# One visit per tile: all of layer 0's other matmuls in a single break of the weighing

## The chip, the cores and the metric

The kernel runs on one core of a Trainium2 chip. Times are device microseconds (us) of one execution. The engines are PE (TensorE; PEld is its weight load), DVE (VectorE), ACT (ScalarE), POOL (GpSimd) and SP (SyncE, which issues most DMAs). Each engine works through its own list of instructions in order and waits on semaphores for the others.

## The reference, cut to what matters

Four graph layers, each followed by a residual sum and a layer norm, on x of 8 batches x 2048 nodes x 64 channels with one 2048 x 2048 adjacency A (a 0/1 mask, each row divided by its sum). The change touches layer 0 and the first steps of layer 1:

```python
# layer 0: Chebyshev terms T0 = I, T1 = A, T2 = 2 A A - I
w = jnp.einsum('nd,dkio->nkio', embedding, weight)   # each node's own weights, D = 16, K = 3
b = jnp.einsum('nd,do->no', embedding, bias)
x_g = jnp.einsum('knm,bmc->bnkc', A_stack, x)
out = jnp.einsum('bnki,nkio->bno', x_g, w) + b
x = layernorm(x + out)
# layer 1, its start
h = x @ W
s = leaky_relu(h @ a_node, 0.2)                      # a score per node and batch
alpha = softmax(where(H.T > 0, s, NEG))              # over the nodes of each of 64 hyperedges
agg = einsum('ben,bnf->bef', alpha, h)
beta = sigmoid((h @ a_gn)[..] + (agg @ a_ge)[..])
industry = (adj / deg) @ (x @ W_ind)
```

## The kernel before, in words

Nodes are taken in 16 tiles of 128 (NT = 16). A first stage (`first_product`, matmul at L492) forms y1 = A x for all tiles, as a mask product in which every fp32 operand is split in a high and a low part (`y_hi`, `y_lo`). Layer 0's loop (`layer0`) then runs over the tiles j = 0 to 16 (the last turn only finishes tile 15).

The bulk of a tile is the *weighing* (`weigh`, matmuls L1109, evacuation L1120): per tile 8 groups g0 to g7; a group multiplies x, y1 and y2 of two batch pairs with the weights of four of the 16 embedding dimensions, on half of the array's rows at a time (64 x 128 weights), into one of two PSUM buffers (`pp`); DVE then adds the four results, each scaled by the node's embedding, to the running sum `r` in four scalar_tensor_tensor instructions. All else is put between the groups by hand, in a fixed list (`program_order` chains every engine's instructions in the order in which they are written):

- after g0, g1, g2: the three steps of the layer norm of tile j - 1 (`normed`, L1128 to L1156); after g1 the first half of POOL's mask scaling of tile j + 1 (`scaled`, L1011 to L1022); after g2 `first_terms` of tile j + 1: y1 transposed (4 matmuls L167), the bias term bp (L1053) from a small load `et`, its copy, and r = x + bias on POOL (L1058).
- after g3: `project` of tile j - 2 (8 matmuls L1197: h and the industry features at once; copies L1216, low part L1217; POOL weights h by the exponential of its score, L1224), the product y2 = A y1 of tile j + 1 (32 matmuls L1072, copy L1078), `to_features` of tile j - 1 (4 transposes, copy L1171), the comparison of the scaled mask with A (`compare`, L1027, DVE), the second half of `scaled` on POOL, and the masks of tile j + 2 (`mask`, L1003, DVE, two of 128 x 1024).
- after g5: the second `compare`, and the low part of the weighted h (`low_part`, L1238, POOL).
- after g6: `second_term` of tile j + 1 (4 transposes of y2, L1088), `scores` of tile j - 1 (8 matmuls L1176 with `wa`, then L1181 to L1188 with the exponential), `gather` of tile j - 2 (2 matmuls L1245).
- after g7: `degrees` of tile j + 1 (1 matmul L1094).

PSUM holds one accumulator for the product, one for the gather, two small buffers (tag `tr`) for transposes and the like, and two `pp` buffers of two banks, which weighing and projection take in turn. In `first_product` seven accumulators (`acc`) are passed around, four for each quarter of the nodes. SP issues the loads (adjacency tile, row scales, x transposed, x) and stores of a tile in the written order too.

The lines of the changed functions and of their callers:

Of the kernel before, what the change touches and what calls it, by code (L numbers as in the profile page):

```python
# [62 lines left out]
def kernel(  # L63
# [168 lines left out]
    def load_w0(pool):  # L232
        w_sb = pool.tile([P, K, D * C], F32, tag="w", name="w0_sb")
        for h in range(2):
            nc.sync.dma_start(w_sb[h * 64:(h + 1) * 64], w0)
        emb_sb = pool.tile([P, NT, D], F32, tag="emb", name="emb_sb")
        nc.sync.dma_start(emb_sb, emb.rearrange("(t p) d -> p t d", p=P))
        bias_sb = pool.tile([D, C], F32, tag="bias", name="bias0_sb")
        nc.sync.dma_start(bias_sb, bias0)
        return w_sb, emb_sb, bias_sb  # L240
# [183 lines left out]
    def first_product(own, pre, rawp, mskp, y_hi, y_lo, prepare):  # L424

        x_hi, x_lo = buffer(own, 0, "x_hi"), buffer(own, 1, "x_lo")
        with tc.tile_pool(name="acc0", bufs=7, space=PSUM) as ps_acc, tc.tile_pool(
# [14 lines left out]

            steps = prepare(ps_s)
# [33 lines left out]
            with program_order():  # L477
                begin(0)
                begin(1)
                for n, (q, i, kk, h) in enumerate(pieces):  # L480
                    begin(n + 2)
                    if i + h == 0:
# [3 lines left out]
                        ]  # L486
                    m = m_of.pop(n)
# [468 lines left out]
    def layer0(  # L956
        own, l0s, rawp, mskp, ps_acc, ps_tr, ps_p, w_sb, emb_sb, bias_sb, bad, deg, y_hi, y_lo,
# [5 lines left out]
        h_sb, wb, wa, vecs, av_sb, pm, es, hgr, aggp, rden, early = layer1s  # L963
        raws, msk, terms, resid, norm, srow = {}, {}, {}, {}, {}, {}
        x1s, xTs, hps, hss, mds = {}, {}, {}, {}, {}

        homes = {"xT": (0, 1, 2), "xs": (3, 4), "hs": (5,), "hsf": (15,), "y1T": (6, 7), "r": (8, 9),
# [23 lines left out]
        def load_x(j):  # L991
            ncols = slice(j * P, (j + 1) * P)
            xT = tile("xT", f"xT_{j}", (P, NP, P))
            nc.sync.dma_start(xT, xt[:, :, ncols])
            et = tile("et", f"et_{j}", (D, P))
            nc.sync.dma_start(et, embt[:, ncols])
            xs = tile("xs", f"xs_{j}")
            nc.sync.dma_start(xs, xn[ncols, :])
            terms[j] = {"x": xT, "et": et, "xs": xs}
# [31 lines left out]

        def first_terms(j):

            tr = ps_tr.tile([P, NP, P], F32, tag="tr", name=f"try1_{j}")
            if j > 1:
                y1 = tile("y1", f"y1_{j}", bufs=1)
                nc.gpsimd.tensor_tensor(y1, y_hi[:, j, :], y_lo[:, j, :], ALU.add)
            for pr in range(NP):
                pc = slice(pr * P, (pr + 1) * P)
                if j > 1:  # L1040
                    transpose(tr[:, pr, :], y1[:, pc])
# [10 lines left out]
            bp = ps_tr.tile([P, QW], F32, tag="tr", name=f"bp_{j}")  # L1052
            nc.tensor.matmul(bp[:, 0:C], terms[j]["et"], bias_sb, start=True, stop=True)  # L1053
            bn = tile("bn", f"bn_{j}", (P, C))
            nc.scalar.copy(bn, bp[:, 0:C])
            r = tile("r", f"r0_{j}")
            for bq in range(2):
                nc.gpsimd.tensor_tensor(  # L1058
                    r[:, 4 * bq * C:4 * (bq + 1) * C]
                    .rearrange("p (h l c) -> p h l c", h=2, l=2),  # L1060
                    swapped(terms[j]["xs"], bq),
                    bn.rearrange("p (h l c) -> p h l c", h=1, l=1).to_broadcast([P, 2, 2, C]),
                    ALU.add,
                )
            resid[j] = r
# [58 lines left out]
        def normed(j, step):  # L1124
            r = resid[j]
            if step == 0:
                s = tile("s", f"s_l0_{j}", (P, B))
# [7 lines left out]
            elif step == 1:  # L1135
                var = tile("var", f"var_l0_{j}", (P, B))
# [8 lines left out]
                std = tile("std", f"std_l0_{j}", (P, B))  # L1145
# [27 lines left out]
        def scores(j):  # L1173
            sp = ps_tr.tile([P, NP, 2, 2], F32, tag="tr", name=f"sgp_{j}")
            for pr in range(NP):
                nc.tensor.matmul(  # L1176
                    sp[:, pr].rearrange("p i h -> p (i h)"), xTs[j][:, pr, :],
                    wa.rearrange("p i h -> p (i h)"), start=True, stop=True,
                )
            sg = tile("sg", f"sg_{j}", (P, NP, 2))  # L1180
            nc.scalar.copy(sg, sp[:, :, 0, :])  # L1181
            nc.scalar.copy(hgr[:, j, 0, :].rearrange("p (r h) -> p r h", h=2), sp[:, :, 1, :])
            ej = es[:, j, :]
            nc.vector.scalar_tensor_tensor(
                ej.rearrange("p (r h) -> p r h", h=2), sg, 0.2, sg, op0=ALU.mult, op1=ALU.max
            )
            nc.vector.tensor_scalar(ej, ej, TOP, None, op0=ALU.min)
            nc.scalar.activation(ej, ej, AF.Exp)  # L1188

        def project(j, h_first=False):  # L1190

            mm = ps_p.tile([P, 2, 2, 4 * C], F32, tag="pp", name=f"hp_{j}")
            mm = mm.rearrange("p h l (m x) -> p h (l m) x", m=2)
            for pr in range(NP):
                for h in range(2):
                    rs = slice(h * 64, (h + 1) * 64)
                    nc.tensor.matmul(  # L1197
                        mm[:, h, pr, :], xTs[j][rs, pr, :], wb[rs], start=True, stop=True
                    )
            if j not in mds:  # L1200
                md = tile("md", f"md_{j}", (P, 2, E))
                nc.gpsimd.tensor_copy(r_(md), pm[:, j, :].unsqueeze(1).to_broadcast([P, 2, E]))
                mds[j] = md.rearrange("p h e -> p (h e)")

            def by_half(t):
                return t.rearrange("p (r h c) -> p h r c", h=2, c=C)


            stay = j >= len(kept_i)
            if stay:  # L1210
# [963 lines left out]
```

## Time and profile before

| what | us |
|---|---|
| median of 3 runs | 1312.41 (1310.28 to 1313.22) |
| span of the profiled execution | 1314.5 |
| first product and preparation | 0 to about 154 |
| layer 0's loop, steady tiles: start of product to start of the next | 33.48 (most), 34.44 (one) |
| product starts of the first tiles | 156.23, 179.43, 210.22, 243.13, 276.63 |
| product start of tile 15 / last matmul of the gather | 645.98 / 714.19 |

The profile comes from one execution, whose own time has no row among the three runs; its span of 1314.5 is 2.1 us above their median. A row of the timeline gives start, length, engine, line, operation, output <- inputs, shape and count of merged instructions; in brackets stands how long the engine was idle before and what ended that. "issue" means that it waited for nothing that the profile shows. A row of the windows gives, for a stretch, the busy time of PE, PEld, DVE, ACT and POOL with instruction counts, then the granted PE clock, the DMA engines' share and GB/s. For an in-order engine the start of one instruction to the start of the next is what a chain is made of; lengths overlap a little.

### The profile page before, as it was taken

To read this page: it belongs to the slowest core of one execution; us is meant where nothing else is said; L and a number is where in the kernel's file an instruction comes from. 1 tells how busy PE (TensorE), PEld (TensorE's weight loads), DVE (VectorE), ACT (ScalarE), POOL (GpSimd) and SP (SyncE) were. 2 spreads that over 40 slices of the span, in tenths; PEclk is the share of its full clock that TensorE was granted. 3 is DMA by queue.
4 is the path that set the end of the run, shared out by engine and by line. 5 is a ranking of instruction groups with operands and counts; after the bars stand their busy time and mean duration, and the time that the engine had idled before them with its cause. 6 is when DMAs were issued, how large, how long until landed. Compare 5 with 4: busy or idle time off the path is not lost. (4 is left out here: it accounts for less than half of the span.)

```text
span 1314.5 us, 19978 instructions
## 1 busy us (share of the span) xinstructions
PE 1253.7 (95%) x7692; PEld 1002.0 (76%) x7692; DVE 886.6 (67%) x1596; ACT 377.9 (29%) x852; POOL 514.4 (39%) x418
## 2 busy tenths in 40 slices
PE   7999799999999999999998599999998899999996
PEld 6777578888888888888886367777766788888885
DVE  5455268888887777887673568877774666665544
ACT  3000001222222222222222356666664521111111
POOL 1000274555554555555411468888872600000000
PEclk9999799999999999999997689999998999999998
DMA  8877833323333333332352212223220133334541
GB/s 293 240 210 149 217 94 105 105 102 102 106 107 107 108 107 107 107 106 82 112 187 75 101 65 97 96 96 97 81 96 1 70 124 128 104 122 152 187 173 67
DMA packets 100792, 157.22 MB, mean 120 GB/s; under 512 B 12881, under 2 KB 64465, under 8 KB 94673
## 3 DMA queue, kind: packets, MB, share of 16 engines
q1 hardware_dynamic: 98208, 151.65, 35.8%
q10 hardware_dynamic: 2304, 4.20, 0.8%
q8 instruction: 63, 1.03, 0.3%
q0 software_dynamic: 176, 0.02, 0.1%
q14 instruction: 41, 0.33, 0.1%
HBM read 118.08 MB, written 37.76 MB: 119 GB/s over the span
## 5 line engine op out<-in xcount | busy, mean ns | idle before, releaser
L1120 DVE SCALAR_TENSOR_TENSOR r<-pp,emb_sb,r 128x256 f32<-128x256 f32 x512 | 247.2, 483 | 105.3 <-PE pp L1109 90.4
L1109 PE MATMUL pp<-w_sb,xT 64*128 64x256 f32 x1024 | 160.6, 390 | 1.8 <-DVE r L1120 1.8
L1109 PE MATMUL pp<-w_sb,y1T 64*128 64x256 f32 x1024 | 153.6, 376 | 0.0
L1109 PE MATMUL pp<-w_sb,y2T 64*128 64x256 f32 x1024 | 153.6, 376 | 0.0
L1058 POOL TENSOR_TENSOR r<-xs,bn 128x256 f32<-128x256 f32 x32 | 22.8, 732 | 245.5 <-issue 213.2
L492 PE MATMUL y1p<-x_hi,m 128*128 128x512 f32 x256 | 107.4, 420 | 7.1 <-ACT x_hi L438 7.1
L1109 PEld LDWEIGHTS pp<-w_sb,xT 64*128 64x128 f32 x1024 | 94.5, 186 | 19.7 <-issue 9.6
L1109 PEld LDWEIGHTS pp<-w_sb,y2T 64*128 64x128 f32 x1024 | 99.8, 187 | 10.8
L1109 PEld LDWEIGHTS pp<-w_sb,y1T 64*128 64x128 f32 x1024 | 99.8, 187 | 10.8
L492 PE MATMUL y1p<-x_lo,m 128*128 128x512 f32 x256 | 104.1, 407 | 0.0
L1072 PE MATMUL y2p<-y_hi,msk 128*128 128x512 f32 x256 | 103.0, 402 | 0.0
L1442 PE MATMUL ind<-y_hi,mj_l 128*128 128x512 f32 x240 | 101.7, 424 | 0.0
L1072 PE MATMUL y2p<-y_lo,msk 128*128 128x512 f32 x256 | 101.3, 396 | 0.0
L1442 PE MATMUL a<-v_hi,mj_l 128*128 128x512 f32 x256 | 100.1, 392 | 0.0
L1442 PE MATMUL a<-v_lo,mj_l 128*128 128x512 f32 x256 | 100.0, 391 | 0.0
L1442 PE MATMUL a<-y_lo,mj_l 128*128 128x512 f32 x240 | 95.1, 396 | 0.0
L1442 PE MATMUL a<-y_hi,mj_l 128*128 128x512 f32 x240 | 94.9, 395 | 0.0
L1442 PE MATMUL ind<-y_lo,mj_l 128*128 128x512 f32 x240 | 94.6, 394 | 0.0
L739 POOL TENSOR_TENSOR ez<-ez,coef 128x1024 f32<-128x1024 f32 x32 | 69.9, 2183 | 56.3 <-DVE ez L737 54.9
L1011 POOL TENSOR_TENSOR ms<-msk,srow 128x1024 f32<-128x1024 f32 x32 | 89.8, 2806 | 4.7 <-DVE ms L1027 4.7
L1003 DVE TENSOR_SCALAR msk<-adj 128x1024 fp32r<-128x1024 f32 x32 | 63.6, 2021 | 9.1 <-DMA adj<-in_at 9.0
L492 PEld LDWEIGHTS y1p<-x_hi,m 128*128 128x128 f32 x256 | 50.2, 196 | 19.6 <-ACT x_hi L438 7.1
(286 smaller groups left out, 2430.3 us busy)
## 6 DMA issues: line engine op xcount, KB each, us to landing
mj_l<-mask SPq DMA_DIRECT2D x46, 1024.0 KB, 4.9
raw<-in_at SPq DMA_DIRECT2D x32, 512.0 KB, 5.0
adj<-in_at SPq DMA_DIRECT2D x64, 256.0 KB, 3.9
mask<-msk SPq DMA_DIRECT2D x32, 512.0 KB, 4.6
xraw<-in_xn SPq DMA_DIRECT2D x8, 512.0 KB, 4.6
oh<-oh SPq DMA_DIRECT2D x32, 128.0 KB, 2.8
xT<-in_xt SPq DMA_DIRECT2D x16, 256.0 KB, 3.2
xs<-in_xn SPq DMA_DIRECT2D x16, 256.0 KB, 2.9
```

The costliest lines, as they stand in the source:

```text
L492: nc.tensor.matmul(accs[q][jj], r_(m[:, t, jj * P:(jj + 1) * P]), r_(part[:, mt, :]), start=i + h + t == 0 and part is x_hi, stop=i == 3 a ...
L739: nc.gpsimd.tensor_tensor(by_b(ez), by_b(ez), per_b(coef, 2 * i, 2), ALU.mult)
L1003: nc.vector.tensor_scalar(r_(m), raws[j][h], 0.0, None, op0=ALU.is_gt)
L1011: nc.gpsimd.tensor_tensor(ms, m, srow[j].unsqueeze(1).to_broadcast([P, 8, P]), ALU.mult)
L1058: nc.gpsimd.tensor_tensor(r[:, 4 * bq * C:4 * (bq + 1) * C] .rearrange("p (h l c) -> p h l c", h=2, l=2), swapped(terms[j]["xs"], bq), bn. ...
L1072: nc.tensor.matmul(acc, r_(msk[j, mt // 8][:, mt % 8, :]), r_(part[:, mt, :]), start=mt == 0 and part is y_hi, stop=mt == NT - 1 and part ...
L1109: nc.tensor.matmul(pp[:, h, pl, :], terms[j][name][rs, 2 * bq + pl], w_sb[rs, k, dq * 4 * C:(dq + 1) * 4 * C], start=k == 0, stop=k == K - 1,)
L1120: nc.vector.scalar_tensor_tensor(rb, ppv[:, :, dd, :], emb_sb[:, j, d:d + 1], rb, op0=ALU.mult, op1=ALU.add)
L1442: nc.tensor.matmul(acc, r_(a[:, mt, :]), r_(part[:, mt, :]), start=mt == 0 and part is hi, stop=mt == NT - 1 and part is lo,)
```

## The change

Layer 0's loop now leaves the weighing once per tile, after g3 (`visit`). In that break stand, in this order: the second half of the projection of tile j - 2 and its score weights, the y1 transposes of tile j + 1, the weighting of tile j - 2, the product of tile j + 1, the transposes of x1 of tile j - 1, the gather of tile j - 2, the y2 transposes of tile j + 1, the degrees of tile j, the first half of the projection of tile j - 1, and at the end the masks of tile j + 2.

- `project` is cut in two halves of two batch pairs each, each with its own `pp` buffer; `wb` has two more columns (W a_node and W a_gn), so that the scores come out of the projection and the matmuls of `scores` and `wa` are gone. The exponential (`weights_of`) and the weighting (`weighted`) follow the projection; the low part is formed at once, in the buffer of y1.
- The bias term of all tiles is formed in 16 matmuls ahead of the first product (`node_bias`), from an embedding loaded whole on ACT's DMA queue into buffers that y_lo takes later; its result takes two of the seven `acc` buffers for a while, and is copied by ACT (`keep_bias`). The per-tile loads of `et`, bp and its copy are gone.
- `first_terms` is cut: `begin_terms` (POOL: y1 = high + low, r = x + bias) after g2, the transposes in the visit. `xs` (x of a tile) has one buffer instead of two and is loaded after `begin_terms`; `ihi` takes the freed one.
- At the end of the loop (j = 16) the second half of tile 15's projection, its weights and the last denominators stand after each other; the buffer of the denominators comes from `tr`.

```diff
+            def node_bias():
+                et, bn_all, rest = bias_in
+                b0 = bn_all[0:D, NT - 1, :]
+                for half in range(2):
+                    bp = ps_acc.tile([P, NT // 2, C], F32, tag="acc", name=f"bp_{half}")
+                    for t in range(NT // 2):
+                        j = half * (NT // 2) + t
+                        nc.tensor.matmul(
+                            bp[:, t, :], et[j // 4][0:D, (j % 4) * P:(j % 4 + 1) * P], b0,
+                            start=True, stop=True,
+                        )
+                    bps.append(bp)
+                rest()
...
+                    if n == 0:
+                        node_bias()
+                    elif n == 1:
+                        keep_bias()
...
-        def scores(j):
-            sp = ps_tr.tile([P, NP, 2, 2], F32, tag="tr", name=f"sgp_{j}")
-            for pr in range(NP):
-                nc.tensor.matmul(
-                    sp[:, pr].rearrange("p i h -> p (i h)"), xTs[j][:, pr, :],
-                    wa.rearrange("p i h -> p (i h)"), start=True, stop=True,
-                )
...
+        def project(j, n, h_first=False):
+            mm = ps_p.tile([P, 2, 2, 4 * C], F32, tag="pp", name=f"hp_{j}_{n}")
+            mm = mm.rearrange("p h l x -> p h (l x)")[:, :, 0:2 * (2 * C + 2)]
+            mm = mm.rearrange("p h (r x) -> p h r x", r=2)
+            for r in range(2):
                 for h in range(2):
                     rs = slice(h * 64, (h + 1) * 64)
                     nc.tensor.matmul(
+                        mm[:, h, r, :], xTs[j][rs, 2 * n + r, :], wb[rs], start=True, stop=True
                     )
...
+            nc.scalar.copy(by_batch(sgs[j]), mm[:, :, :, 2 * C])
+            nc.scalar.copy(by_batch(hgr[:, j, 0, :]), mm[:, :, :, 2 * C + 1])
...
+        def weights_of(j):
+            ej, sg = es[:, j, :], sgs[j]
+            nc.vector.scalar_tensor_tensor(ej, sg, 0.2, sg, op0=ALU.mult, op1=ALU.max)
+            nc.vector.tensor_scalar(ej, ej, TOP, None, op0=ALU.min)
+            nc.scalar.activation(ej, ej, AF.Exp)
...
-            hss[j] = tile("hs", f"hs_hi_{j}"), hs
-            nc.scalar.copy(r_(hss[j][0]), hs)
...
+            hi, lo = tile("hs", f"hs_hi_{j}"), tile("y1", f"hs_lo_{j}", bufs=1)
+            nc.scalar.copy(r_(hi), hs)
+            nc.gpsimd.tensor_tensor(r_(lo), hs, hi, ALU.subtract)
+            hss[j] = hi, lo
...
+        def visit(j):
+            when(j - 2, project, 1)
+            when(j - 2, weights_of)
+            when(j + 1, first_terms)
+            when(j - 2, weighted)
+            if j + 1 < NT:
+                for _ in product(j + 1):
+                    pass
+            when(j - 1, to_features)
+            when(j + 1, compare, 0)
+            when(j + 1, scaled, 1)
...
+            when(j - 2, gather)
+            when(j + 1, second_term)
+            when(j, degrees)
+            when(j - 1, project, 0, j == NT)
+            when(j + 2, mask, 0)
+            when(j + 2, mask, 1)
...
                     elif g == 3:
-                        when(j - 2, project)
-                        if j + 1 < NT:
-                            for _ in product(j + 1):
-                                pass
-                        when(j - 1, to_features)
-                        when(j + 1, compare, 0)
-                        when(j + 1, scaled, 1)
...
-                        when(j + 2, mask, 0)
-                        when(j + 2, mask, 1)
+                        visit(j)
                     elif g == 5:
                         when(j + 1, compare, 1)
-                        when(j - 2, low_part)
...
-                    elif g == 6:
-                        when(j + 1, second_term)
-                        when(j - 1, scores)
-                        if j < NT:
-                            when(j - 2, gather)
-                        else:
-                            project(NT - 1, h_first=True)
-                            denominators(NT - 1, NT)
-                            gather(NT - 2)
...
+                    elif g == 6 and j == NT:
+                        project(NT - 1, 1, h_first=True)
+                        weights_of(NT - 1)
+                        weighted(NT - 1)
+                        denominators(NT - 2, NT)
...
-                    elif g == 7:
-                        when(j + 1, degrees)
```

## The prediction

> **What bounds it now.** I read the page's busy shares first, then the span by slices, then busy time by windows.
>
> ```profile
> span 1314.5 us, 19978 instructions
> ...
> PE 1253.7 (95%) x7692; PEld 1002.0 (76%) x7692; DVE 886.6 (67%) x1596; ACT 377.9 (29%) x852; POOL 514.4 (39%) x418
> ...
> PE   7999799999999999999998599999998899999996
> ```
>
> ```profile
> 410.61:444.09 33.48, 33.48 (x267) 28.25 (x265) 26.82 (x50) 7.56 (x15) 17.86 (x15) 1.00 0.32 105
> ```
>
> The window is one tile of layer 0's loop: 33.48 us, all PE, at full clock; DVE has work for 26.82, POOL for 17.86. So an interruption of PE costs its length, and DVE has 6.7 us to spare, but only if it can use them. The timeline of the same tile shows one interruption:
>
> ```profile
> 427.02 0.60 PE L1109 MATMUL pp<-w_sb,y2T 64*128 64x256 f32 x4
> ...
> 427.55 0.42 PEld L167 LDWEIGHTS try<-ident,y 128*128 128x128 f32 x4 [0.33 <-issue]
> 427.55 0.65 PE L167 MATMUL try<-ident,y 128*128 128x128 f32 x4
> ...
> 428.04 0.95 PE L1176 MATMUL sgp<-wa,xT 128*128 128x4 f32 x8
> ...
> 429.49 0.30 PEld L1109 LDWEIGHTS pp<-w_sb,xT 64*128 64x128 f32 x4 [0.36 <-issue]
> 429.49 0.70 PE L1109 MATMUL pp<-w_sb,xT 64*128 64x256 f32 x4
> ```
>
> The reader is to see the engine change from weighing (64 rows) to transposes, scores and gather (128 rows) and back, with "issue" gaps at both ends: nobody is waited for, the change itself takes that time. Weighing matmuls start in pairs, 0.216 us apart (the starts of the rows: 427.02 to 427.24). On leaving, the next start comes after 0.31 (427.24 to 427.55); on return the first pair takes 0.32 (429.49 to 429.81). This interruption thus costs 429.49 - 427.45 (where the next pair would have started) + 0.10 = 2.14. By the same reckoning the four of a tile cost 1.15 (after group g2), 9.07 (after g3), 2.14 (after g6) and 0.40 (after g7), 12.77 in all; eight groups of 12 pairs x 0.2157 = 2.59 us are 20.7. The sum, 33.47, is the tile.
>
> **PE after the change.** T = 0 is the first projection matmul of the only visit. From the rows' starts: half a projection, 4 pairs by 0.11 and 0.21 to the next kind, 0.54; y1 transposes to 1.1; product 7.22 from first to last start, so 8.3; transposes of x1 to 8.9; the gather's two at 9.0 and 9.3. Here sits the added wait: the y2 transposes need ACT's copy of y2p, which starts 0.49 after the last product matmul and takes 0.69: 9.5. The transposes and the gather cover it. y2 transposes 9.55 to 9.93, degrees 10.04, the other half projection 10.24 to 10.67, weighing again at 10.85. Gone are sgp (8 by 0.112 = 0.9), bp (0.36) and three round trips (about 0.3 each, 0.9), less 0.2 for splitting the projection. Two more columns on 128 are nothing. **PE alone would need 10.85 + 20.7 = 31.55.**
>
> **DVE after the change.** Instruction order per engine shows what matters more: both masks (L1003, today behind compare, under the product) now stand behind y2T and the second half of lo. They cannot start before PE has all but finished its visit, and g4's four evacuations (L1120, 2.04) queue behind them. PE has two pp buffers, so g6 waits for g4's evacuation. How long a mask takes depends on POOL:
>
> ```profile
> 142.45 0.69 DVE L1003 TENSOR_SCALAR msk<-adj 128x1024 fp32r<-128x1024 f32 x1 [8.71 <-DMA adj<-in_at]
> ```
>
> ```profile
> 413.89 3.37 POOL L1011 TENSOR_TENSOR ms<-msk,srow 128x1024 f32<-128x1024 f32 x1
> ...
> 414.94 4.58 DVE L1003 TENSOR_SCALAR msk<-adj 128x1024 fp32r<-128x1024 f32 x2
> ...
> 417.22 1.75 POOL L1015 TENSOR_TENSOR cs<-msk 128x512 f32<-128x512 f32 x1
> ```
>
> 0.69 with POOL silent; the pair takes 4.58 beside POOL: the first ends 0.6 after POOL's ms, the second 0.55 after POOL's cs. So a mask waits out the POOL operation that is running and then needs 0.6. A rule of the Trainium skill (SBUF — State Buffer, section "SBUF: two separate sides") speaks against the new place: VectorE and GpSimd share a port pair that is locked for a whole instruction. By the rule at its worst both masks would wait out a whole ms of 2.36, 5.9 for the pair, and the period below would be 36.3; by the rows it depends on which POOL operation runs at that moment, so that is worked out next.
>
> POOL's own chain: scores arrive with the projection; copies of scores, ihi, h to 1.6; DVE is busy with g3's evacuation to 2.9, then lo, es to 3.6; exp 3.9 (its table load, 1.28, is over by then); hs waits for compare (1.24, to 4.9; beside each other compare took 1.56 instead of 1.22 at 413.44), then 1.04; hs_hi 0.62; hs_lo 1.27: 7.9, in time for the gather at 9.3. Then scaled: 2.36, 1.30, 0.74, 0.46, 0.45 from 7.9 to about 13.3. On DVE: y2T starts 0.31 after the last y2 transpose, 10.24; lo needs ACT's half ihi (11.6): masks from 12.05. POOL is in its third, short operation; mask one ends near 12.97, mask two waits 0.46 for the next and ends near 13.98. g4 evacuates 13.95 to 15.99; PE's g6 starts at 16.14 (0.147 after DVE's end, the distance in 675.73 to 675.87), 0.1 late. g5 to 18.0, compare 1.27, g6 19.27 to 21.31. PE's next g0 can start 21.46. From there DVE's g0, normalization steps and g1, g2 follow by 3.28 and 2.54 (435.39, 438.67, 441.21 in the trace), slower than PE's 2.59 a group, so PE waits as it does in the last tile of the trace:
>
> ```profile
> 672.60 0.70 PE L1109 MATMUL pp<-w_sb,xT 64*128 64x256 f32 x4 [0.29 <-DVE r L1120]
> ...
> 675.87 0.70 PE L1109 MATMUL pp<-w_sb,xT 64*128 64x256 f32 x4 [0.41 <-DVE r L1120]
> ```
>
> DVE g0 24.26, g1 27.54, g2 30.08 to 32.12; PE's g3 starts 29.73 and ends 32.32. **The period is 32.3**, not 31.55, and every microsecond that DVE is later from y2T to g4 comes on top. Bounds for the masks: 1.4 (POOL silent) and 4.65 (as beside ms and cs); I take 1.9, nearest to the short POOL operations that lie there. Both ends stay in the range: 32.2 and 35.0.
>
> **Outside the steady tiles.** Twelve periods (tile 2's visit to tile 14's) x (32.3 - 33.48) = -14.2. First bp (0.33), a switch less in tile 0 and one easier period (32.91 now): -2.0. Tile 14, no masks: -1.3. Tile 15's visit has no product: the gather of 13 waits for exp, hs, hs_hi, hs_lo, about 6.9 us after the projection, where now it lies three groups later:
>
> ```profile
> 680.88 1.04 POOL L1224 TENSOR_TENSOR hs<-h,es 128x512 f32<-128x512 f32 x1 [24.64 <-ACT h L1216]
> ...
> 681.96 0.62 ACT L1231 CAST hs_hi<-hs 128x512 fp32r<-128x512 f32 x1 [1.21 <-POOL hs L1224]
> ...
> 682.65 1.26 POOL L1238 TENSOR_TENSOR hs_lo<-hs,hs_hi 128x512 fp32r<-128x512 f32 x1 [0.73 <-ACT hs_hi L1231]
> ```
>
> Weighing resumes at 8.05; the last evacuation ends 20.65 after T against 17.27 now (678.54 to 695.81): +3.4. PE idles some 4 us there. Behind 2.16 us of idling (152.5 to 154.7) the trace has product matmuls at 0.43 instead of 0.23 for 3.4 us; a like stretch at g4 would add up to 3.4, nothing is the other end: +4.5 in all. The Trainium skill (TensorE: Matmul & The Clock Gate, "Part 1: The HAM clock gate") has a whole idle window of about 3.4 us throttle the clock; a pause of 4 us holds one only now and then, so by the rule this term would mostly be +3.4, while the row shows half speed behind a shorter pause. In the tail, exp of 14 and 15 now follows the projection, and 14's table load (1.28) lies on the way: +2 (0 to 4). At the start, 16 small matmuls stand ahead of y1p, which starts at 7.07; one bp (two instructions) takes 0.36 warm, so up to 5.8 in all, of which the part before 7.07 is free once et has landed (its queue issues from 0.8, some 0.4 for each of five loads, and 1.5 us to landing in the page's issue table's row for et: about 4.5): 5.8 - 2.6 = 3.2 at most. The product's own cold start, 0.43 instead of 0.23 a matmul until 13.1, may shorten by as much: +1.5 (0 to 4). bp also takes two of seven acc buffers, so the second quarter's product waits for three evacuations, not one: +0.5. Bias formation, wa's memset, the et loads: off the path, nothing; SP has 16 loads fewer. xs with one buffer is loaded a tile ahead.
>
> Sum: -14.2 - 2.0 - 1.3 + 4.5 + 2 + 2 = -9.0: 1305.5 against the span of 1314.5. The runs' median, 1312.41, lies 2.1 below this span: **1303.4**.
>
> **Rivals.** (B) Slower: DVE becomes the bound. If POOL's scaled is later by 3 to 4 us (hs chain late), the masks meet ms and cs as today: 4.65, period 35.0, 12 x 1.5 = +18, no gain in tiles 0 and 1, the ends as above: 1338. It decides from 0.75 us of delay a tile on; 1.8 us gives 1316. For: POOL's order, the 4.58 row. Against: POOL is done with ms 1.7 us before the masks. (C) PE alone is the bound, DVE's lag is absorbed: 31.55, 12 x -1.93, small ends: 1290. Against: the waits at 672.60 and 675.87. (D) The loop gains half (7), the ends cost 10: no change, 1311 to 1313.
>
> **Numbers.** Forecast 0.55 (1296 to 1310), B 0.25 (1314 to 1338), C 0.08, D 0.12. Range 1290 to 1328: C's end, and B to two thirds. A measurement tells about 0.2% (2.6 us) apart: faster 0.60, same 0.13, slower 0.27.
>
> **What would show it.** Right: tile periods near 32.3; PE idle before L1138's g1 to g3 groups put to DVE; masks behind y2T with a sum near 2 us; a PE gap of 4 us in tile 15's visit. Wrong: masks still 4.6 (B), periods of 31.6 (C), try2 waiting for y2 by more than 0.2, or a clock below 1.00 inside the loop.

## The result, and the profile after

The changed kernel takes 1319.36 us (median of four runs, 1318.44 to 1319.78), the kernel before 1312.55 beside it (1310.28 to 1313.22): ratio 1.0055, 95% interval 1.0042 to 1.0068. It is **slower by about half a per cent**. The forecast was 1303.4; the range held the time, the direction was wrong.

The page of the changed kernel, its span, busy shares, and PE and its clock by slices:

```profile
span 1317.6 us, 19736 instructions
...
PE 1235.5 (94%) x7564; PEld 1004.8 (76%) x7564; DVE 847.7 (64%) x1612; ACT 381.7 (29%) x902; POOL 510.9 (39%) x417
...
PE   7999899999999999999988699999998899999997
...
PEclk9999899999999999999987689999998999999999
```

PE has 18 us less to do than before (1235.5 against 1253.7), yet the span grew. The time went into waits. The weighing's group on the page (busy time, mean ns of one, idle time just before it and what ended it):

```profile
L1109 PE MATMUL pp<-w_sb,xT 64*128 64x256 f32 x1024 | 160.6, 390 | 1.8 <-DVE r L1120 1.8
```

```profile
L1138 PE MATMUL pp<-w_sb,xT 64*128 64x256 f32 x1024 | 161.2, 386 | 18.2 <-issue 8.7
```

The first row is from the kernel before, with 1.8 us of idle time; after the change it is 18.2. Where they lie shows in busy times by windows, each window one period, from the product of one tile to the next (columns: window and length, then busy time of PE, PEld, DVE, ACT and POOL, granted clock, DMA share, GB/s). First the two periods from tile 3's product on, then a late one:

```profile
247.21:280.91 33.70, 31.86 (x259) 28.07 (x257) 24.64 (x52) 7.72 (x19) 17.62 (x16) 1.00 0.33 104
280.91:316.72 35.81, 33.56 (x258) 29.61 (x257) 25.30 (x51) 7.71 (x19) 17.60 (x16) 0.95 0.30 98
548.16:580.70 32.54, 31.86 (x258) 28.10 (x257) 23.49 (x50) 7.71 (x19) 17.61 (x16) 1.00 0.33 108
```

The late period, 32.54, is near the forecast's 32.3. But an early one takes 33.70 and the next 35.81, **longer than before the change** (33.48). What they have more is on DVE: 52 and 51 instructions instead of 50. The timeline of DVE in the longer one, and of PE (two rows):

```profile
297.92 1.45 DVE L1056 SCALAR_TENSOR_TENSOR ms<-ms,adj 128x1024 f32<-128x1024 f32 x1
299.31 0.08 DVE L1056 DVE_READ_ACCUMULATOR ms<-ms,adj 128x1 f32 x1
299.31 1.91 DVE L260 TENSOR_REDUCE flagbox<-pm 128x64 f32<-128x1024 f32 x1
301.15 4.17 DVE L1149 SCALAR_TENSOR_TENSOR r<-pp,emb_sb,r 128x256 f32<-128x256 f32 x8
```

```profile
303.28 0.70 PE L1138 MATMUL pp<-w_sb,xT 64*128 64x256 f32 x4 [2.18 <-issue]
...
305.59 1.13 PE L1138 MATMUL pp<-w_sb,y1T 64*128 64x256 f32 x4
```

Line 260 belongs to `lists_flag` (lines 245 to 288), a generator in which the kernel checks its input lists; behind g5 of each of the tiles 1 to 7 one step of it runs on DVE. The evacuations of g6 and g7 queue behind it, and PE, which has two pp buffers, stands 2.18 us before the next tile's g0. "issue" is named as releaser, but what PE waited for is the buffer: the row at 301.15 holds eight evacuations, and with the fourth, near 303.2, g6's buffer is free. Afterwards the clock is at half for 3.41 us (four matmuls of a row take 1.13 instead of 0.63).

The kernel before has the same step in the same place, and its period shows nothing of it: PE is busy for the whole 33.56 us. There PE leaves the weighing after g6 (at 292.57) and after g7 (at 297.31), so that g6's evacuation, 295.18 to 297.21 behind line 257 (260 after the change), is done before the next tile's g0 needs the buffer:

```profile
276.63:310.19 33.56, 33.56 (x268) 28.67 (x266) 28.47 (x50) 7.45 (x15) 17.97 (x16) 1.00 0.31 106
```

```profile
293.33 1.93 DVE L257 TENSOR_REDUCE flagbox<-pm 128x64 f32<-128x1024 f32 x1
```

This table is worked out from the starts in the traces; of the kernel before there is a second profile (`control_before`). For the changed kernel the first row is a mean of nine profiles, its own and those of eight variants that form the bias at the same place (158.98 to 161.55); the other rows are its own. The denominators are the first matmul into `denp` behind the weighing of tile 15; `he` is what is formed from the gathered sums.

| stretch (us) | before, two profiles | after | forecast | found |
|---|---|---|---|---|
| start to tile 0's product | 156.23, 153.41 | 160.2 | +1.7 | +5.3 |
| to tile 3's product | 86.90, 87.87 | 88.23 | -1.7 | +0.8 |
| twelve periods, to tile 15's product | 402.85, 402.84 | 398.59 | -14.2 | -4.3 |
| to the denominators (tiles 14, 15) | 47.67, 47.65 | 52.61 | +3.2 | +5.0 |
| to the transposes of he | 24.55, 21.93 | 24.12 | +2 | +0.9 |
| rest | 596.34, 595.51 | 595.03 | 0 | -0.9 |
| sum | | | -9.0 | +6.8 |

The sum is the difference of the medians. The third row lost 10 us of its forecast; the first, second and fourth cost 8 us more; the last two gave 2 back.

### The profile page after: what moved, and what is told of

Read it like the earlier page. It is cut to its first block, busy times and chain, and to the rows that moved or that the text cites. A ratio compares the mean times of both kernels' runs of the same rounds, so it can differ in the third digit from the quotient of the medians.

```text
span 1317.6 us, 19736 instructions
## 1 busy us (share of the span) xinstructions
PE 1235.5 (94%) x7564; PEld 1004.8 (76%) x7564; DVE 847.7 (64%) x1612; ACT 381.7 (29%) x902; POOL 510.9 (39%) x417
## 4 chain that ended last, share of the span: by engine, by line
PE 82%; DVE 9%; issue 3%; ACT 2%; DMA 2%; POOL 1%; ACTq 0%; SPq 0%; DVEq 0%; POOLq 0%
PE pp L1138 20%; PE a L1487 18%; PE y2p L1101 9%; PE ind L1487 9%; PE y1p L521 8%; DVE r L1149 5%; PE fc L836 3%; PE df L845 2%; PE hp L1218 1%; PE gp L736 1%; PE try L167 1%; PE yp L1581 1%; PE trm L167 1%; PE red L777 1%; PE dp L756 1%
## 5 line engine op out<-in xcount | busy, mean ns | idle before, releaser
L1138 PE MATMUL pp<-w_sb,xT 64*128 64x256 f32 x1024 | 161.2, 386 | 18.2 <-issue 8.7
L1138 PE MATMUL pp<-w_sb,y1T 64*128 64x256 f32 x1024 | 158.2, 379 | 0.0
L1138 PE MATMUL pp<-w_sb,y2T 64*128 64x256 f32 x1024 | 158.1, 379 | 0.0
L1138 PEld LDWEIGHTS pp<-w_sb,xT 64*128 64x128 f32 x1024 | 101.5, 188 | 35.5 <-PE pp L1138 17.4
L1138 PEld LDWEIGHTS pp<-w_sb,y1T 64*128 64x128 f32 x1024 | 106.4, 189 | 6.3
L1138 PEld LDWEIGHTS pp<-w_sb,y2T 64*128 64x128 f32 x1024 | 106.2, 189 | 6.3
L1068 POOL TENSOR_TENSOR r<-xs,bn_all 128x256 f32<-128x256 f32 x32 | 22.9, 736 | 209.8 <-issue 189.6
L1040 POOL TENSOR_TENSOR ms<-msk,srow 128x1024 f32<-128x1024 f32 x32 | 83.1, 2597 | 14.9 <-DMA srow<-s_row 7.3
L1162 ACT ACTIVATE sq_l<-r 128x512 f32<-128x512 f32 x16 | 10.1, 631 | 266.9 <-DVE r L1158 266.9
L1117 DVE TENSOR_TENSOR y2T<-try,xT 128x512 f32<-128x512 f32 x16 | 11.1, 692 | 95.3 <-PE try L167 95.3
```

The lines of the kernel that those rows point to most:

```text
L1040: nc.gpsimd.tensor_tensor(ms, m, srow[j].unsqueeze(1).to_broadcast([P, 8, P]), ALU.mult)
L1068: nc.gpsimd.tensor_tensor(r[:, 4 * bq * C:4 * (bq + 1) * C] .rearrange("p (h l c) -> p h l c", h=2, l=2), swapped(terms[j]["xs"], bq), bn_ ...
L1138: nc.tensor.matmul(pp[:, h, pl, :], terms[j][name][rs, 2 * bq + pl], w_sb[rs, k, dq * 4 * C:(dq + 1) * 4 * C], start=k == 0, stop=k == K - 1,)
```

## The experiments

Theory: **late VectorE**. From y2T to the next tile's g2 DVE's chain sets the pace; whatever stands on it there, in single tiles too, delays PE. The start and tile 15 cost what they cost separately. Rivals: the long early periods have another cause; or merging itself is what hurts. All edits are to the changed kernel if nothing else is said; ratios are to the kernel before.

| kernel | us | ratio, 95% interval | period late in the loop |
|---|---|---|---|
| changed kernel | 1319.36 | 1.0055, 1.0042 to 1.0068 | 32.54 |
| e1_flags_visit | 1312.00 | 0.9988, 0.9979 to 0.9997 | 32.53 |
| e2_flags_late | 1320.78 | 1.0056, 1.0039 to 1.0073 | 33.7 to 34.4 |
| e4_masks_early | 1326.53 | 1.0100, 1.0085 to 1.0116 | 33.26 |
| e6_compare_visit | 1306.51 | 0.9955, 0.9942 to 0.9969 | 32.17 |
| e8_scattered | 1349.88 | 1.0280, 1.0266 to 1.0295 | 34.8 to 36.4 |
| e10_scattered_split | 1327.14 | 1.0112, 1.0094 to 1.0131 | 33.53 |
| e3_gather_late | 1318.61 | 1.0040, 1.0026 to 1.0054 | 32.55 |
| e7_tile15 | 1313.92 | 1.0011, 1.0000 to 1.0023 | 32.54 |
| e5_bias_in_wait | 1311.40 | 0.9990, 0.9981 to 0.9999 | 32.54 |
| e9_all | 1292.25 | 0.9839, 0.9824 to 0.9853 | 32.17 |
| e11_norm_spread | 1294.92 | 0.9878, 0.9855 to 0.9900 | 32.26 |

### The list checks: moved into the visit, and to later tiles

```
 in visit:      when(j + 1, compare, 0)
+               if j:
+                   next(flags, None)
 behind g5:     when(j + 1, compare, 1)
-               if j:
-                   next(flags, None)
```

> The changed kernel, except that the step of the list checks (lines 252 to 288, one in each of the tiles 1 to 7) is taken inside the visit, behind the first compare, where VectorE waits 5.75 us for the y2 transposes, and no longer behind g5. Theory (late VectorE): in the changed kernel VectorE is at the end of the path from y2T to the next tile's g2, so these steps (0.45 to 1.9 us each) delay the next tile's g0. The starts of the product from tile 2's to tile 9's are 33.42, 33.70, 35.81, 33.98, 34.18, 32.96 and 32.70 apart, and 32.54 afterwards: the excess is 9.0 us in all. It should go but for some tenths: periods 32.5 to 32.7 in these tiles, full clock in tile 4, some 1310.5 us, ratio to the kernel before 0.997 to 0.999. Rival (the early periods are long for another reason, as cold starts, PE's own switches or loads that are late): 1317 to 1320, ratio 1.004 to 1.006, the same periods as before the move.

Measured: 1312.0. The same two periods as above, now in this kernel:

```profile
249.19:281.73 32.54, 31.88 (x259) 28.10 (x257) 24.36 (x52) 7.71 (x19) 17.59 (x16) 1.00 0.33 107
281.73:314.28 32.55, 31.85 (x258) 28.07 (x256) 25.45 (x51) 7.71 (x19) 17.60 (x16) 1.00 0.32 108
```

The same 52 and 51 instructions are there, DVE is as busy, and the periods are 32.54 and 32.55. From tile 0's product to tile 15's it takes 478.31 instead of 486.82: 8.5 us less. The seven steps sum to 8.5 us on DVE in the changed kernel, but that the two agree so well is in part chance: 1.4 us are the half clock behind line 260, since the same period takes 34.38 in the next variant, which has the step and full clock.

The counterpart, `if j >= 8` in place of `if j` at the old place:

> The changed kernel, except that the steps of the list checks start in tile 8 instead of tile 1 (behind g5, as they were). Late VectorE: the excess moves with the steps. Periods of 32.5 to 32.7 from the product of tile 3 to that of tile 9; from tile 9's product on 33.4 to 35.8 in the order in which 33.42, 33.70, 35.81, 33.98, 34.18, 32.96 came; the time stays within 2 us of 1319. Rival (the early tiles are slow in themselves): the periods stay where they were, and only some tenths are added later.

Measured: 1320.78. Periods of 32.52 to 32.55 from tile 3's product to tile 9's, then 33.66, 33.67, 34.38, 33.97, 34.16, 32.95. The excess follows the steps. Both rivals to this point are out: the early tiles are not slow in themselves.

### What else is on DVE's chain: masks, compare, normalization

```
 in visit:      when(j + 1, compare, 0)
+               when(j + 2, mask, 0)
+               when(j + 2, mask, 1)
 ...
                when(j - 1, project, 0, j == NT)
-               when(j + 2, mask, 0)
-               when(j + 2, mask, 1)
```

> The changed kernel, except that the two masks of tile j + 2 stand on VectorE behind the first compare, under the product (where the kernel before has them), and not behind y2T and the second half of lo. Theory (late VectorE): the two masks cost 1.5 us (559.18 to 560.67) on the path from y2T to g4; taken off it, PE becomes the bound in the steady tiles: the period falls from 32.54 to between 31.6 and 32.0, and the list checks' steps lose 0.5 to 1 us each of their harm too. 14 tiles: 8 to 15 us less, 1304 to 1311, ratio 0.994 to 0.999. Masks beside POOL take longer there (4.58 for the pair in the kernel before), which fits into 5.75 us of idle time. Rival (they do not fit: POOL's hs, ms and cs and the masks hold each other up, y2T or hs_lo come late and PE waits in the visit): period 32.5 or more, 1318 to 1330.

Measured: 1326.53, the theory's number missed by far. Rows of a late tile, first of this variant (g4's evacuation, POOL's y1, the second compare), then of the changed kernel (g5's evacuation, the second compare, POOL's y1):

```profile
563.32 2.04 DVE L1149 SCALAR_TENSOR_TENSOR r<-pp,emb_sb,r 128x256 f32<-128x256 f32 x4 [1.34 <-PE pp L1138]
...
567.71 1.27 POOL L1065 TENSOR_TENSOR y<-y_hi,y_lo 128x512 f32<-128x512 f32 x1
567.87 2.20 DVE L1056 SCALAR_TENSOR_TENSOR ms<-ms,adj 128x1024 f32<-128x1024 f32 x1
```

```profile
563.20 2.05 DVE L1149 SCALAR_TENSOR_TENSOR r<-pp,emb_sb,r 128x256 f32<-128x256 f32 x4 [0.49 <-PE pp L1138]
...
565.16 1.47 DVE L1056 SCALAR_TENSOR_TENSOR ms<-ms,adj 128x1024 f32<-128x1024 f32 x1
...
565.50 2.25 POOL L1065 TENSOR_TENSOR y<-y_hi,y_lo 128x512 f32<-128x512 f32 x1
```

With the masks gone from there, DVE waits 1.34 us for PE's g4. But in the changed kernel, too, DVE is idle for 0.49 us before g5's evacuation, until PE has finished g5: the masks had delayed nothing behind it. And early masks let POOL be early: its y1 now starts 0.16 us before the second compare and no longer 0.34 after it, and the compare takes 2.20 instead of 1.47. PE's gap before the next tile's g0 (start to start) grows by as much, from 739 to 1468 ns, and the period by 0.72. The chain thus begins at g5's evacuation, not at y2T, and the compare is on it. So that was taken off, on top of e1 (`es` in the expectation is the exponential of the scores, `hs` is h weighted by it):

```
 in visit:      when(j - 2, weighted)
+               if j:
+                   when(j, compare, 1)
 behind g5:
-               when(j + 1, compare, 1)
```

> As e1_flags_visit (list checks in the visit), and the second compare of a tile (1.47 us behind g5) is moved as well, into the next tile's visit behind es, where VectorE waits 5.75 us. Theory (from g4 to the next g2, VectorE has 8 evacuations of 2.04, the compare and the normalization, and that chain is the steady bound): the period falls by at least 0.9 from 32.54, to 31.5 to 31.7, where PE alone is the bound; 13 tiles: 1299 to 1302, ratio 0.989 to 0.992. Rival (PE's waits come from the two pp buffers and the normalization alone, or the compare beside POOL's hs holds hs_lo up, or the adjacency buffers, freed later, make the masks late): period 32.2 or more, 1308 to 1318.

Measured: 1306.51, period 32.17: right in kind, two fifths of the gain in size. One wait of PE in a late tile is left, before g3 (3.65 before the next product's start; the expectation below for e11_norm_spread calls it g2):

```profile
564.06 0.70 PE L1138 MATMUL pp<-w_sb,xT 64*128 64x256 f32 x4 [0.39 <-DVE r L1149]
```

From start to start this gap is 762 ns where 216 would be the rhythm, so 0.55 is lost: g3 needs the buffer of g1, whose evacuation stands behind DVE's sums and centring of the tile before (0.67 and 0.69). 32.17 less 0.55, less 0.1 before g6, is 31.5: what PE alone would need by this account, and the forecast had 31.55; no run reached it. In the changed kernel there are two such gaps, 739 and 696 ns, before the next tile's g0 (its buffer is g6's, evacuated behind the compare) and g3 (behind the normalization): 0.52 and 0.48, together what 32.54 has over 31.55. The last of them, before g3, was to go in a variant of e9_all (which follows below):

```
 behind g0: sums    behind g1: + centring, square    behind g2: variance
 in visit, behind es: + scaling to x1, then r0 of the next tile (POOL)
```

> As e9_all, but the normalization of the tile before is spread: sums behind g0, centring behind g1, variance behind g2, scaling in the visit behind es, with POOL's start of the next residual behind it. In e6_compare_visit PE still waits 0.55 a tile before g2, behind sums and centring (0.67 and 0.69), which stand together. Theory (VectorE's lag is a sum over neighbouring groups against a slack of 0.55 a group): with 2.72 a group instead of 3.4, 2.7 and 3.0 the wait vanishes, the period falls from 32.17 to 31.5 to 31.7, 13 tiles: 1284 to 1287, ratio 0.977 to 0.980. Rival (the later POOL work delays hs_lo or the masks, or trx waits for x1): 32.1 or more, 1291 to 1297.

Measured: 1294.92, against 1292.25 without it (ratios 0.9878 and 0.9839): the rival. The wait before g3 is gone, but POOL's r0 (the start of the next tile's sum r) comes later, so the masks meet POOL's cs and take 2.53 for the pair instead of 1.79, and PE waits before g6:

```profile
540.30 2.53 DVE L1032 TENSOR_SCALAR msk<-adj 128x1024 fp32r<-128x1024 f32 x2
542.76 3.66 DVE L1151 SCALAR_TENSOR_TENSOR r<-pp,emb_sb,r 128x256 f32<-128x256 f32 x7
```

```profile
544.94 0.70 PE L1140 MATMUL pp<-w_sb,xT 64*128 64x256 f32 x4 [0.66 <-DVE r L1151]
```

This is rival B of the prediction, in small: masks that meet POOL's additions.

### Merging undone

```
 in visit:   - when(j - 2, gather), when(j + 1, second_term), when(j, degrees)
             + both halves: when(j - 2, project, 0), when(j - 2, project, 1)
 behind g6:  + when(j + 1, second_term), when(j - 2, gather)
 behind g7:  + when(j + 1, degrees)
```

> The changed kernel with its merging undone, all else kept (bias ahead, scores as columns): y2's transposes and the gather are back behind g6, the degrees behind g7 (tile 0's behind g1), both half projections stand together at the start of the stretch behind g3, and so the masks lie under the product again. Theory (late VectorE): an interruption of PE is also a pause in which VectorE catches up, so three interruptions more cost PE some 0.9 us less 0.2 for the unsplit projection (31.55 to about 32.25), but VectorE's chain no longer sets the end and the list checks are hidden, and the gather of 13 waits for nothing in tile 15. Steady period 32.2 to 32.6, no long tiles early, some 9 us less for the checks, 4 to 5 for tile 15: 1303 to 1308, ratio 0.993 to 0.997, so faster than the changed kernel. Rival (the merging is what brought the 0.94 us of a period): period 33.2 to 33.5, 1314 to 1320.

Measured: 1349.88, far off both. The edit brought a wait of its own; the second half projection (x8, the first half had gone at 567.74) waits for the pp buffer that g3's evacuation still reads:

```profile
570.48 0.72 PE L1218 MATMUL hp<-wb,xT 64*128 64x130 f32 x8 [2.10 <-DVE r L1149]
```

So the projection must be split over two places once it fills two pp buffers, which is a reason for the split that I had missed. Mended, with the split as in the changed kernel:

> As e8_scattered, but the projection stays split as in the changed kernel (first half at the end of the stretch behind g3, second half at the start of the next one). In e8_scattered the second half waits 2.1 us for VectorE's evacuation of g3 (568.11 to 570.48), which the scattering itself does not need. Theory (an interruption of PE is also a pause for VectorE): period 32.2 to 32.6, list checks hidden, 1302 to 1308, ratio 0.992 to 0.996. Rival (the merging is what brought the gain of the period): 33.2 to 33.5, 1314 to 1320.

Measured: 1327.14, period 33.53: the rival. PE is busy 32.33 us of it, against 31.86 with one visit, and idle 1.2. The largest part of that is again a lost cover, the projection waiting for ACT's copy of the x1 transposes, with no gather and no y2 transposes between:

```profile
558.84 0.60 PE L167 MATMUL trx<-ident,x 128*128 128x128 f32 x4
560.31 0.72 PE L1218 MATMUL hp<-wb,xT 64*128 64x130 f32 x8 [0.88 <-ACT xT L1200]
```

So the merged order is 1.0 us a period shorter than this scattered one, and my idea that scattered breaks cost nothing because DVE catches up in them is wrong for the period as a whole. The parts: 0.5 us more work of PE and the 0.88 us of this wait, less the wait before g0 (0.52 in the changed kernel), which is gone here. DVE does catch up in the breaks behind g6 and g7. So how much of the 1.0 us is due to the breaks themselves and how much to the lost cover is open: no run has the breaks scattered and that copy covered. The idea is right for the list checks: here they lengthen the early periods by 0.5 at most (33.55, 33.95, 33.54, 34.01, 33.97 from tile 3's product on, 33.53 later).

### Tile 15

```
 in visit:      if j != NT - 1:
                    when(j - 2, gather)
 behind g6:     if j == NT - 1:
                    gather(j - 2)
```

> The changed kernel, except that in tile 15 the gather of tile 13 is left out of the visit and comes after g6, where its inputs have long been ready. Theory (uncovered gather): the visit of tile 15 has no product to cover exp, hs, hs_hi and hs_lo, PE stands idle from 678.3 to 682.6 and then works at half clock from 683.4 to 690.3. The stretch from there to the denominators goes from 21.1 to some 16 us (15.1 in the kernel before): 5 us less, 1314.4, ratio 1.001 to 1.003. Rival (the wait is only passed on: the next thing in the visit, the half projection of 14, waits for the copy of the transposes, or VectorE's lo and g4 become the end): PE still waits 3 us or more there and the gain is under 2 us, 1317.5 to 1319.5.

Measured: 1318.61, the rival. ACT in the changed kernel, and PE in this one:

```profile
681.94 0.62 ACT L1264 CAST hs_hi<-hs 128x512 fp32r<-128x512 f32 x1 [1.15 <-POOL hs L1257]
682.46 0.58 ACT L1200 COPY xT<-trx 128x512 f32<-128x512 f32 x1
```

```profile
679.50 0.25 PE L1123 MATMUL dgp<-ones_r,both 128*128 128x2 f32 x1
684.27 1.24 PE L1218 MATMUL hp<-wb,xT 64*128 64x130 f32 x8 [4.51 <-ACT deg L1126]
```

ACT runs in order, and the copy of the x1 transposes stands behind the cast of hs_hi, which waits for exp and hs. The gather was only the first to wait; the projection behind it waits as long, 4.51 us, and then works at half clock (1.24 for eight). So in tile 15 the transposes, degrees and half projection went ahead of es, and the gather to the last visit:

```
 in visit:   + if j == NT: gather(j - 3)
             + if j == NT - 1: to_features(j - 1); degrees(j); project(j - 1, 0)
               when(j - 2, weights_of)
               (the old places are left out for j == NT - 1)
```

> The changed kernel, except that in tile 15 the transposes of x1 of tile 14, the degrees and the first half projection of 14 come before es, exp and hs of tile 13, and the gather of 13 is put to the start of the last visit. Theory (in e3_gather_late the wait was passed on to the half projection, because ACT's copy of the transposes stands behind the cast of hs_hi, which waits for exp and hs): PE's idle time in tile 15's visit falls from 4.5 to 1.5 us or less, no half clock follows, and from the product of tile 15 to VectorE's last evacuation it takes 50 us instead of 54.8: 4 to 5 us less, 1314.5, ratio 1.001 to 1.003. Rival (what is gained there is given back in the tail, where VectorE, ACT and POOL set the pace): 1317 to 1319.5.

Measured: 1313.92, 5.4 us less. PE waits 1.50 for g3's evacuation and weighs on, at full clock:

```profile
680.54 0.72 PE L1218 MATMUL hp<-wb,xT 64*128 64x130 f32 x8 [1.50 <-DVE r L1149]
681.06 0.63 PE L1138 MATMUL pp<-w_sb,xT 64*128 64x256 f32 x4
```

From tile 15's product to the denominators it is 45.3 instead of 52.6 (47.7 before the change): 7.3 less in these two profiles. Their spans differ by 6.4, the medians by 5.4.

### The start

```
-                    if n == 0:
+                    if n == 30:
                         node_bias()
-                    elif n == 1:
+                    elif n == 31:
                         keep_bias()
```

> The changed kernel, except that the bias matmuls stand before the matmuls of piece 30 of the first product (of 32), not of piece 0, and ACT's copies before piece 31's; the et buffers are then held until there. There PE waits for the first masks of layer 0 (143.79 to 147.75 in the changed kernel, 136.85 to 143.52 in the kernel before). Theory (the start costs 3 to 6 us, since all of the first product moved from 7.07 to 16.3 and that wait gives back only a part): y1p starts at some 7 to 8, the 32 instructions lie in the wait, and tile 0's product starts at 156 to 157.5 instead of the 159.0 to 161.6 of the changed kernel and the four kernels run after it: 2.5 to 5 us less, 1314.5 to 1317, ratio 1.001 to 1.003. Rival (the transfers set that moment whatever PE does): tile 0's product starts at 159 or later and the time stays at 1318 to 1320.

Measured: 1311.40, 8 us less than the changed kernel, more than expected. PE in the changed kernel (the bias, and the wait late in the first product):

```profile
9.32 7.05 PE L454 MATMUL bp<-bn_all,et 16*128 16x64 f32 x32 [9.32 <-DMA bn_all<-in_bias]
...
147.75 0.42 PE L397 MATMUL sm<-tri,pT 64*128 64x64 f32 x1 [3.57 <-DVE oh L420]
```

and in this one:

```profile
7.93 0.79 PE L521 MATMUL y1p<-x_hi,m 128*128 128x512 f32 x1 [7.93 <-ACT x_hi L441]
...
135.60 3.78 PE L454 MATMUL bp<-bn_all,et 16*128 16x64 f32 x32
```

The bias matmuls wait for bias0's transfer until 9.32 and take 7.05 us, since PE's clock is still low: they start 213 ns apart, at piece 30 112 ns, and the profile grants the full clock from 21.24 on (13.36 in the kernel before). So y1p starts at 16.31 instead of 7.07. At piece 30 they take 3.78, lie where PE waited for the first mask's transfer (DVE's oh, which releases PE there, stands behind that mask), and tile 0's product starts at 152.08. That is earlier than in the kernel before (156.23, 153.41), whose first visit also formed a bias of its own.

> The kernel before, unchanged. Its first profile had a span of 1314.5, which stands for a time of 1316.2 if the time is the span and 1.75, as in the profile of the changed kernel (1319.34 and 1317.6): 3.7 above its median. Expected if that was chance: a span of about 1311, periods of 33.48 again, the list checks invisible in them, and the 3 us found in the first product or the tail. If it was not chance: a span of 1314 again.

Measured: a span of 1309.2 and a time of 1310.95. The periods from tile 1's product on are the same to 0.01, line by line, the one of 34.44 included; the first profile was 2.8 us later at tile 0's product, 1.0 shorter from there to tile 1's, and took 2.6 more in the tail. Those were chance, so a sum against one profile carries some 5 us of it.

### All of it

> The changed kernel with the list checks and the second compare in the visit (as e6_compare_visit), the bias at piece 30 (as e5_bias_in_wait) and the order of tile 15 (as e7_tile15). If the three causes are separate, the ratios' differences from the changed kernel add up: 0.9955, less 1.0055 - 0.9990 = 0.0065, less 1.0055 - 1.0011 = 0.0044, gives 0.9846, or 1292; expected 1290 to 1296, period 32.17. If they share a cause (one wait shrinks when another does, or an earlier start only lengthens a later wait for a transfer), less: 1297 to 1303.

Measured: 1292.25 with ratio 0.9839, where the sum of the parts said 0.9846. The parts add up, so the causes are separate, and this version beats both kernels, the one before by 1.6%:

```profile
span 1292.5 us, 19748 instructions
...
PE 1228.3 (95%) x7564; PEld 1003.1 (78%) x7564; DVE 860.6 (67%) x1612; ACT 379.7 (29%) x900; POOL 501.8 (39%) x417
...
PE   7999999999999999999997599999998899999996
```

DVE is busy for longer than in the changed kernel (860.6 against 847.7 us), and the kernel is 2% faster: the gain comes from the order, not from less work.

## Why the prediction was wrong, point by point

- **The failed step: "Twelve periods (tile 2's visit to tile 14's) x (32.3 - 33.48) = -14.2".** It multiplies a steady tile. The terms that it left out or mis-sized: the list checks in six of these periods, +8.1 (398.59 less 12 x 32.54; some 1.4 of it is the half clock that followed one of them), which the text never named though they stand behind g5 in the kernel; the steady period itself, 32.54 for 32.3, +2.9. The kernel before took 1.1 more than 12 x 33.48, mostly in one period of 34.44, where the step of tile 6 puts a matmul (line 274 there) between two weighing groups; this is a gain of 1.1 against the forecast. Sum: -4.3, as in the table. The prediction even had the rule, "every microsecond that DVE is later from y2T to g4 comes on top"; it was not asked which instructions stand on DVE in only some tiles. e1_flags_visit and e2_flags_late show the cause: the excess goes when these steps leave the place behind g5, and follows them to other tiles. Before the change their DVE instructions cost nothing: the control's periods are 33.50, 33.56, 33.47, 33.50 with them and 33.48 without.
- **"The period is 32.3"**: right in kind (DVE's chain, waits before groups of the next tile), 0.24 short. The working has PE wait 0.1 before g6, 0.14 before g0 (21.46, where 16.14 and two groups give 21.32) and 0.50 before g3 (29.73 for 29.23); measured were nothing, 0.52 and 0.48. So the wait before g3 was right, and the mis-sized one is g0's. The working lets DVE evacuate g5 from 15.99 on, although by its own times PE ends g5 only at 16.03, and puts the compare to 1.27; in the trace DVE waits 0.49 for PE's g5, and the compare takes 1.47. So the chain starts at g5's evacuation, and "every microsecond that DVE is later from y2T to g4 comes on top" does not hold for small delays: e4_masks_early took the masks away from there and gained nothing.
- **"PE alone would need 31.55"**: the account of e6_compare_visit agrees, 31.5.
- **Masks 1.9 for the pair**: 1.57 in the changed kernel's steady tiles; neither 4.65 nor the 5.9 of the rule's worst case came. Rival B did not occur; e11_norm_spread shows it in small. (Its "1.8 us gives 1316" is a slip: at 12 periods, 1.8 us a tile on 1303.4 give 1325.)
- **y2's transposes are covered**: right in steady tiles, wrong in tiles 0 and 1, which have no gather and, in tile 0, no x1 transposes to cover ACT's copy. These two waits, 1.24, are half of what the second row of the table is short by (2.5, where a gain of 1.7 had been forecast); the list check of tile 1 is most of the rest (33.42 to tile 3's product, 32.28 in e1_flags_visit):

```profile
190.48 0.66 PE L167 MATMUL try<-ident,y 128*128 128x128 f32 x4 [0.84 <-ACT y L1107]
...
222.22 0.66 PE L167 MATMUL try<-ident,y 128*128 128x128 f32 x4 [0.40 <-ACT y L1107]
```

- **Start, "+1.5 (0 to 4)"** and "+0.5": +5.3. The bias's own transfer was put to "about 4.5" from a row for a load on another queue; it came at 9.32. And the 32 instructions ran at a low clock (7.05, not 5.8). e5_bias_in_wait, with tile 0's product at 152.08, shows the place of the bias to be worth 8 us.
- **Tile 15, +4.5 with the clock**: mechanism right (PE idle 4.0 and 0.9 us, then half clock from 683.4 to 690.3), found +6.0 (23.23 from T to the last evacuation's end, 677.34 to 700.57, against 17.27): the idle time and most of the clock's part came true together, and the copy of the x1 transposes queues behind the same wait, which the prediction did not see.
- **Tail, "+2"**: +0.9, within the scatter that the control shows.

The chance of 0.27 for slower rested almost wholly on rival B (0.25). A rival for "an instruction that I did not list becomes visible when the slack goes" was missing.

## What to carry to other kernels

When an edit spends an engine's slack, list every instruction on that engine between the two waits that bound it, for every tile and not for a steady one: setup checks, first and last tiles, branches. Merging the breaks of PE shortened the steady tile at once here (32.54 for 33.48), but it also took away the pauses in which DVE caught up; about half of the 27 us between the changed kernel and e9_all came from moving DVE's work as well (e6_compare_visit, 1306.51), into the stretch where PE is busy with something that DVE does not feed: the same list checks cost 8 us behind g5 and nothing under the product. Before new matmuls are put first in a program, look for a wait that exists already and put them there.

## What the runs showed of the hardware

- A wait of PE of the same length led to half clock in some kernels and not in others. In e8_scattered a wait of 2.10 us stands in every steady tile; behind six of them the clock was at half for 3.41 us. Two neighbouring periods, one without and one with it:

```profile
500.36:535.17 34.81, 32.39 (x259) 27.40 (x257) 23.80 (x49) 7.72 (x19) 16.65 (x15) 1.00 0.31 102
535.17:571.54 36.37, 33.94 (x258) 28.54 (x257) 23.80 (x49) 7.70 (x19) 15.61 (x15) 0.95 0.30 96
```

  The gap behind line 260, 2.56 us from start to start, was followed by 3.41 us at half clock in the changed kernel and e5_bias_in_wait, and not in e2_flags_late, e3_gather_late and e7_tile15 (2.53 there); a gap of 3.26 in e4_masks_early was not. All half-clock stretches of these traces that end before the kernel does last 3.41 us or a multiple. The Trainium skill (TensorE: Matmul & The Clock Gate, "Part 1: The HAM clock gate") has a window of about 3.4 us that runs freely, which fits the multiples and the chance; that a whole idle window is needed, as the page has it, does not fit, since a wait of 2.2 us holds none. The measurement decides.
- A DVE compare of 128x1024 in a steady tile takes 1.22 at its quickest, 1.45 to 1.51 behind g5 in the changed kernel, 2.06 beside POOL's hs (e6_compare_visit) and 2.20 where POOL's y1 had started first (e4_masks_early); where the compare started first it took 1.47, and y1 2.25 instead of 1.27. A mask pair takes 1.57 in the changed kernel, 2.53 in e11_norm_spread and 4.58 in the kernel before. In these rows the time of a DVE instruction goes with what POOL runs at that moment, so moving one also re-times the others.
